# Where a doubled bias is added to an accumulator: on VectorE in eight pieces, or on GpSimd in four

## The chip, the cores and the metric

The kernel runs on one core of a Trainium2 chip. The metric is device time in microseconds (us), from the launch of the program to its end on the core. A core has five engines with an instruction queue each: TensorE (matrix products; PE in the profile, with the loading of weights shown apart as PEld), VectorE (DVE), ScalarE (ACT), GpSimd (POOL) and SyncE (SP, which here only starts transfers). TensorE writes its results to PSUM; the other working memory is SBUF. A queue is worked through in order, and an instruction waits on semaphores for what it needs from other engines and from transfers.

## What is computed

Cut to what matters, with x of 1024 x 512, weight of 64 x 512 x 512, all in fp32:

```python
out_lin = x @ lin_w.T + lin_b
xv = einsum('bf,efm->bem', x, weight)
zp = einsum('bf,efm->bem', square(x), square(weight))
interaction = 0.5 * sum(square(xv) - zp, axis=1)
return out_lin + interaction
```

Per embedding e there is one product of x with a 512 x 512 matrix; the squares of all 64 products are summed. The sum over e of zp is one product of square(x) with the sum of the squared weights. The bias lin_b has 512 elements, one for each output column.

## The kernel before, in words

**Accumulator.** Two SBUF tiles, `acc[0]` and `acc[1]`, hold the upper and lower half of the output rows (index r), each as 128 partitions x 2 (j, blocks of 128 rows) x 2 (s, further blocks of rows) x 512 columns. They hold twice the result: the linear part is written to them doubled (lines 226, 303, 309), the squares are added, and the last stage multiplies by 0.5 (lines 688 and 713). So the bias too is added doubled.

**Main loop.** The 64 embeddings are worked in 16 groups q of 4. In a group the products are formed by a seven-product scheme (as Strassen's) at two levels: the outer blocks "1" to "7" each have an x side, made once, and a weight side, made by GpSimd for every group (`outer_t`, line 380; `inner_t`, lines 391, 393, 395). A `unit` (line 413) is one outer block i and one row half j: seven products on TensorE (line 421) into three PSUM banks x, v and y, ScalarE copies bank x into bank y (line 475), and VectorE adds the banks to what other units left in z tiles (lines 446, 457, 458 and the joins of line 467). For block "5" GpSimd adds two more pieces per j (`rest`, line 472). There are 14 units in a group. ScalarE squares the finished z tiles (`squares`, line 497), and a transfer from GpSimd's queue that adds to its destination gathers them into acc (`gather`, line 506). Squared weights are made by ScalarE (line 515) and summed in the same way (line 522). SP's queue loads the weights of the next group (line 358).

**What sets the order.** A timetable, written out by hand. Every step is put into `Stream` with a time (`st.at(t, fn)`), group q starts at 98q, and `run()` (line 23) issues all steps sorted by time. The times only set the order of the instructions in each engine's queue; when one runs is decided by its semaphores. One step of the timetable is one product. Near the change, on GpSimd's queue, in times from the start of a group: the gathers of z place "c" into acc[0] at 38.8 and 52.9, the inner weight sums of block "3" (tp, t6, t4) at 57.9, 58 and 61.7, the weight-sum transfer at 61.6, the two `rest` additions of the first j at 67 and 69.8, the gather of "c" into acc[1] at 73, the two `rest` additions of the second j at 74 and 76.8. The last gathers of the group before into acc[0] come at 12.3, into acc[1] at 26.2.

**The bias.** SP loads it, repeated over 128 partitions, into the SBUF tile `bias` (line 350, time -1). In groups 1 to 4 (n from 0 to 3) VectorE adds `2.0 * bias` to one piece of 128x512 of acc[0] at 27.6 and to one of acc[1] at 41.6 (`add_bias`, line 348); n gives the piece, j = n // 2 and s = n % 2. Eight instructions in all.

**The end.** After the last group comes the product of the squared x with the summed squared weights (lines 659 and 722), and stores.

Of the kernel before, what the change touches and what calls it, by code (L numbers as in the profile page):

```python
# [9 lines left out]
AF = mybir.ActivationFunctionType  # L10
ALU = mybir.AluOpType
# [17 lines left out]
def kernel(  # L29
# [31 lines left out]
    nc = tc.nc  # L61
    _, _, _, Q = x.shape
    E, F, M = weight.shape
    P = 128
# [16 lines left out]
    acc = [  # L81
        const.tile([P, 2, 2, M], F32, tag=f"acc{r}", name=f"acc{r}") for r in range(2)
    ]
# [26 lines left out]
    st = Stream()  # L110
# [232 lines left out]

    bias = const.tile([P, M], F32, tag="bias", name="bias")

    def add_bias(r, j, s):
        o = acc[r][:, j, s]
        nc.vector.scalar_tensor_tensor(o, bias, 2.0, o, ALU.mult, ALU.add)  # L348

    st.at(-1, lambda: nc.sync.dma_start(bias, lin_b.partition_broadcast(P)))  # L350

    for n in range(4):
        for r, t in enumerate((27.6, 41.6)):
            st.at(98 * (n + 1) + t, lambda r=r, n=n: add_bias(r, n // 2, n % 2))

    def load_w(q, kk, v):
        src = weight[4 * q + 2 * v : 4 * q + 2 * v + 2]
# [177 lines left out]
    for q in range(NQ):  # L535
# [29 lines left out]
        for k, n, r, times in (  # L565
# [5 lines left out]
            for j in range(2):  # L571
                t = g0 + 14 * k + 7 * j + 14.6
# [259 lines left out]
```

## Time and profile before

| | |
|---|---|
| time, median of 3 runs | 1425.74 us (1425.23 to 1425.85) |
| the profiled execution's own time | 1423.9 us |
| its span, first to last instruction | 1422.1 us |
| mean granted TensorE clock | 0.996 |
| TensorE busy | 1407.7 us (99%), 3340 instructions |
| VectorE busy | 893.6 us (63%), 1271 |
| ScalarE busy | 620.8 us (44%), 824 |
| GpSimd busy | 1248.8 us (88%), 812 |
| transfers that add z to acc (line 506) | 190 issues, median 8.5 us to landing for 512 KB |
| load of the bias (line 350) | 1 issue, 256 KB, 13.5 us to landing |

The profile is of one execution, so sums of its durations are to be set against 1423.9 us. A line of a timeline gives the start, the duration, the engine, the line of the code, the operation, output<-inputs by tile name, the shapes, and in brackets how long the engine had been idle before and what released it. In the list of waits the numbers are the total in us, how often, and the longest. A product of fp32 shows as two matmul records. Ends of matmuls are modelled, so successive records overlap.

### The profile page before, as it was taken

How to read it: one execution, taken by the hardware profiler on the slowest of the kernel's cores; microseconds unless marked ns; L12 is line 12 of the kernel's file. 1: busy time of each engine (PE TensorE's matmuls, PEld its weight loads, DVE VectorE, ACT ScalarE, POOL GpSimd, SP SyncE). 2: the span in 40 equal slices, each digit the busy share in tenths (PEclk: the TensorE clock that was granted, in tenths of full speed). 3: DMA queues.
4: the chain of work that ended last, by engine and by line, in shares of the span. 5: the costliest groups of instructions: out<-in, count | busy, mean ns of one | idle time of the engine just before them, and what ended most of it. 6: DMA issues, size and time to landing. Idle time of an engine off the chain costs nothing.

```text
span 1422.1 us, 11166 instructions
## 1 busy us (share of the span) xinstructions
PE 1407.7 (99%) x3340; PEld 636.5 (45%) x3340; DVE 893.6 (63%) x1271; ACT 620.8 (44%) x824; POOL 1248.8 (88%) x812
## 2 busy tenths in 40 slices
PE   9999999999999999999999999999999999999999
PEld 5444444444444444444444444444444444444446
DVE  6665667657576565665656566565666656566665
ACT  2444353443534435344443534534353443534443
POOL 7988789888898888979989898988989988898984
PEclk9999999999999999999999999999999999999999
DMA  5299898898888998997998899898998998899885
GB/s 214 59 222 191 200 197 160 200 195 195 197 163 206 196 206 193 182 238 156 230 195 197 204 181 234 166 232 178 191 233 160 225 195 211 186 184 237 163 189 133
DMA packets 58108, 273.63 MB, mean 192 GB/s; under 512 B 5440, under 2 KB 8000, under 8 KB 41792
## 3 DMA queue, kind: packets, MB, share of 16 engines
q0 software_dynamic: 36432, 198.20, 71.1%
q1 hardware_dynamic: 21328, 74.19, 15.3%
q10 hardware_dynamic: 288, 0.52, 0.1%
q8 instruction: 27, 0.44, 0.1%
q14 instruction: 33, 0.27, 0.1%
HBM read 72.61 MB, written 2.10 MB: 53 GB/s over the span
## 4 chain that ended last, share of the span: by engine, by line
PE 94%; DMA 2%; issue 1%; POOL 1%; DVE 1%; ACT 0%; POOLq 0%
PE y L421 39%; PE x L421 26%; PE v L421 25%; DMA acc<-z 2%; PE lin L216 1%; PE y_last L659 1%; DVE acc L348 1%; PE v_last L659 0%; PE x_last L659 0%; POOL t L380 0%; PE y_lin L271 0%; DMA t<-lin_wT 0%; POOL t L395 0%; PE v_lin L271 0%; PE x_lin L271 0%
## 5 line engine op out<-in xcount | busy, mean ns | idle before, releaser
L421 PE MATMUL y<-t,xs 128*128 128x512 f32 x896 | 424.0, 594 | 10.3 <-DVE z L467 9.6
L475 ACT COPY y<-x 128x512 f32<-128x512 f32 x224 | 127.7, 570 | 623.1 <-PE x L421 623.0
L467 DVE TENSOR_TENSOR z<-y,s 128x512 f32<-128x512 f32 x192 | 132.7, 691 | 238.0 <-PE y L421 238.0
L421 PEld LDWEIGHTS y<-t,xs 128*128 128x128 f32 x896 | 169.7, 190 | 226.7 <-issue 202.8
L506 POOL DMA_DIRECT2D acc<-z x190 | 213.2, 1153 | 64.3 <-DMA acc<-z 62.7
L497 ACT ACTIVATE z<-z 128x1024 f32<-128x1024 f32 x256 | 260.1, 1054 | 11.8 <-POOL z L472 9.3
L421 PE MATMUL x<-w,xs 128*128 128x512 f32 x512 | 252.0, 600 | 0.0
L421 PE MATMUL y<-tp,xs 128*128 128x512 f32 x448 | 229.1, 593 | 0.0
L421 PE MATMUL v<-tp,xs 128*128 128x512 f32 x448 | 228.8, 592 | 0.0
L472 POOL TENSOR_TENSOR z<-z,s 128x1024 f32<-128x1024 f32 x64 | 149.6, 2355 | 50.7 <-DVE s L467 50.7
L421 PE MATMUL x<-t,xs 128*128 128x512 f32 x384 | 188.3, 592 | 0.0
L391 POOL TENSOR_TENSOR tp<-w 128x1024 f32<-128x1024 f32 x64 | 175.2, 2738 | 13.9 <-PE y L421 12.6
L467 DVE TENSOR_TENSOR z<-v,s 128x512 f32<-128x512 f32 x192 | 132.8, 691 | 72.2 <-PE v L421 70.6
L458 DVE TENSOR_TENSOR z<-y,z 128x512 f32<-128x512 f32 x192 | 132.4, 690 | 57.4 <-PE y L421 57.4
L380 POOL TENSOR_TENSOR t<-w,t 128x1024 f32<-128x1024 f32 x64 | 164.1, 2725 | 0.0
L458 DVE TENSOR_TENSOR z<-x,z 128x512 f32<-128x512 f32 x192 | 132.3, 689 | 37.3 <-PE x L421 35.7
L421 PEld LDWEIGHTS x<-w,xs 128*128 128x128 f32 x512 | 98.4, 192 | 123.8 <-issue 123.5
L391 POOL TENSOR_TENSOR tp<-t 128x1024 f32<-128x1024 f32 x48 | 139.5, 2906 | 0.0
L421 PEld LDWEIGHTS y<-tp,xs 128*128 128x128 f32 x448 | 85.6, 191 | 107.8 <-issue 107.8
L421 PEld LDWEIGHTS v<-tp,xs 128*128 128x128 f32 x448 | 85.1, 190 | 107.3 <-issue 104.2
L421 PE MATMUL v<-w,xs 128*128 128x512 f32 x256 | 130.7, 592 | 0.0
L446 DVE TENSOR_TENSOR s<-v,z 128x512 f32<-128x512 f32 x160 | 110.6, 691 | 27.8 <-PE v L421 27.1
(113 smaller groups left out, 1485.0 us busy)
## 6 DMA issues: line engine op xcount, KB each, us to landing
w<-weight SPq DMA_DIRECT2D x64, 1024.0 KB, 12.8
acc<-z POOLq DMA_DIRECT2D x128, 512.0 KB, 8.5
w_sum<-w_sb POOLq DMA_DIRECT2D x63, 1024.0 KB, 10.2
acc<-z POOLq DMA_DIRECT2D x62, 1024.0 KB, 8.7
w<-x SPq DMA_DIRECT2D x2, 1024.0 KB, 10.2
out<-z SPq DMA_DIRECT2D x7, 256.0 KB, 2.3
xs<-x SPq DMA_DIRECT2D x2, 384.0 KB, 6.9
t<-lin_wT ACTq DMA_DIRECT2D x2, 256.0 KB, 4.2
```

The lines of the kernel that those rows point to most:

```text
L216: nc.tensor.matmul(LIN[n], quarter(0, kk, (0, 1, 3, 2)[2 * s + l])[:, ts(j, P)], lw_sb[:, 2 * kk + l, :], start=(kk == 0 and l == 0), stop ...
L348: nc.vector.scalar_tensor_tensor(o, bias, 2.0, o, ALU.mult, ALU.add)
L380: nc.gpsimd.tensor_sub(OUTER[i][:, u], a[:, u], b[:, u])
L391: nc.gpsimd.tensor_sub(t, b[:, 1], b[:, :, 0])
L421: nc.tensor.matmul(d[bank], xsl(i, o)[:, ts(j, P)], operand_b(q, i, o), start=start, stop=True, skip_group_check=True,)
L446: nc.vector.tensor_add(o, d[bank], zblk(q, addend, j, b))
L458: nc.vector.tensor_add(zblk(q, dst, j, b), d[bank], zblk(q, addend, j, b))
L467: nc.vector.tensor_add(s if both else zblk(q, dst, j, b), d[bank], s)
L472: nc.gpsimd.tensor_add(place(q, n)[:, 1, j], place(q, src)[:, 1, j], d["s"])
L475: st.at(t0 + 0.5, lambda: nc.scalar.copy(d["y"], d["x"]))
L497: lambda u=u: nc.scalar.activation(z[:, u, j], z[:, u, j], AF.Square),
L506: nc.gpsimd.dma_start(o, z, accum_op=ALU.add)
```

## The change

The tile `bias` is doubled in place, once, by ScalarE at time 21. The addition to acc moves from VectorE to GpSimd: in place of eight instructions of 128x512 at 27.6 and 41.6 there are four of 128x1024 at 64.5 of groups 1 to 4, each for one r and one j and both s, with the bias read twice over by a step of 0. n now gives r = n // 2 and j = n % 2. The load of the bias stays as it is.

```diff
-    def add_bias(r, j, s):
-        o = acc[r][:, j, s]
-        nc.vector.scalar_tensor_tensor(o, bias, 2.0, o, ALU.mult, ALU.add)
+    def add_bias(r, j):
+        o = acc[r][:, j]
+        nc.gpsimd.tensor_add(o, o, bias.unsqueeze(1).broadcast_to([P, 2, M]))
 
     st.at(-1, lambda: nc.sync.dma_start(bias, lin_b.partition_broadcast(P)))
+    st.at(21, lambda: nc.scalar.activation(bias, bias, AF.Copy, scale=2.0))
 
     for n in range(4):
-        for r, t in enumerate((27.6, 41.6)):
-            st.at(98 * (n + 1) + t, lambda r=r, n=n: add_bias(r, n // 2, n % 2))
+        st.at(98 * (n + 1) + 64.5, lambda n=n: add_bias(n // 2, n % 2))
```

## Prediction

> **What bounds the kernel now.** I read the page's busy shares first, then the waits of TensorE, then the lines that the diff removes, then the timelines around one of them. The shares:
>
> ```profile
> PE 1407.7 (99%) x3340; PEld 636.5 (45%) x3340; DVE 893.6 (63%) x1271; ACT 620.8 (44%) x824; POOL 1248.8 (88%) x812
> ```
>
> TensorE is the bound; a change elsewhere counts only where TensorE waits for it. Its waits are few:
>
> ```profile
> PE y L421 <- DVE z L467: 9.6, 4, 2.7
> PE y_spin L202 <- PEq L821: 0.8, 1, 0.8
> PE y L421 <- POOL t L395: 0.7, 1, 0.7
> ```
>
> So four gaps, 9.6 us in all, wait for a VectorE join (L467). What makes that join late is the removed line:
>
> ```profile
> L348 DVE SCALAR_TENSOR_TENSOR acc<-bias,acc x8: 1371/3518/5667, 138.3 to 414.0; 128x512 f32<-128x512 f32 x8
> ```
>
> Eight of them, 1.37 to 5.67 us each, where VectorE's other 128x512 operations take 0.69. Around the second one (VectorE, then TensorE, then GpSimd; columns: start, duration in us, engine, line):
>
> ```profile
> 149.63 0.69 DVE L458 TENSOR_TENSOR z<-x,z 128x512 f32<-128x512 f32 x1 [0.17 <-PE x L421]
> 150.24 5.31 DVE L348 SCALAR_TENSOR_TENSOR acc<-bias,acc 128x512 f32<-128x512 f32 x1
> 155.47 0.68 DVE L467 TENSOR_TENSOR z<-y,s 128x512 f32<-128x512 f32 x1
> ```
>
> ```profile
> 152.86 1.02 PE L421 MATMUL y<-t,xs 128*128 128x512 f32 x2
> 156.20 1.20 PE L421 MATMUL y<-t,xs 128*128 128x512 f32 x2 [2.32 <-DVE z L467]
> 157.19 3.55 PE L421 MATMUL x<-w,xs 128*128 128x512 f32 x4
> ```
>
> ```profile
> 150.22 1.56 POOL L395 TENSOR_TENSOR t<-w,t 128x512 f32<-128x512 f32 x1
> 151.44 1.18 POOL L522 DMA_DIRECT2D w_sum<-w_sb  x1
> 152.04 2.94 POOL L391 TENSOR_TENSOR tp<-t 128x1024 f32<-128x1024 f32 x1
> ```
>
> L348 starts at 150.24, just behind GpSimd's L395 (150.22), and ends at 155.55, about 0.6 us after GpSimd's L391 (154.98): it stood still while GpSimd worked, then did its 0.69 us. The join queued behind it came at 155.47, TensorE had a gap of 2.32 us, and the next four matmuls took 3.55 us where four in a row elsewhere take 1.88.
>
> **What the Trainium skill says.** "SBUF — State Buffer", section "Who interferes with whom": a VectorE instruction with two SBUF inputs contends with a GpSimd instruction that reads SBUF, and the later one blocks until the first is done; with at most one SBUF input (and outside the two-port modes) it does not contend. The trace agrees: L348 reads bias and acc, both in SBUF, and stretches to 5.31 us; the joins and sums read one operand from PSUM and hold 0.69 us. It goes a little beyond the page: the 0.26 us between L395's end (151.78) and L391's start did not let L348 in. "TensorE: Matmul & The Clock Gate", section "What's actually happening", makes the clock depend on how busy the array has been; the slow matmuls after the gap agree, and the page's clock is otherwise full.
>
> **What each stall costs.** The ScalarE copy y<-x (L475) runs once per unit of seven products, so its starts in ScalarE's timeline are a ruler:
>
> ```profile
> 144.48 0.57 ACT L475 COPY y<-x 128x512 f32<-128x512 f32 x1 [3.47 <-PE x L421]
> ...
> 150.49 0.57 ACT L475 COPY y<-x 128x512 f32<-128x512 f32 x1 [1.63 <-PE x L421]
> 160.78 0.57 ACT L475 COPY y<-x 128x512 f32<-128x512 f32 x1 [9.72 <-PE x L421]
> ```
>
> A unit takes 6.01 us (144.48 to 150.49), but the one with L348 takes 10.29: 4.28 lost. The other three such units read from the same timeline are 9.96 (and 6.31 for the unit after it), 8.58 and 10.44: 4.25, 2.57 and 4.43 lost. Sum 15.53. Cross-check: the first copies of weight groups 1 to 5 stand at 114.44, 202.84, 291.21, 377.90 and 466.77, so those four groups take 352.33 us; groups 5 to 9 take 84.12 each, four of them 336.48. Difference 15.85, of which 0.32 is a wait in group 4 for GpSimd. So the removal can return about 15.5 us.
>
> **The change, part by part.**
> (a) Removed: 8 VectorE L348. The first of each group (1.37 to 1.75 us) makes no TensorE gap: worth nothing. The second makes all four gaps: minus 15.5 us. What is late next there? In groups 5 to 15 the same place runs without L348 at 6.01 us per unit, so nothing is waiting behind it.
> (b) Added: one ScalarE activation on bias, 128x512. ScalarE's acc<-lin rows of this form take 0.60 us; "ScalarE: Activation LUTs", section "What ACT_TABLE_LOAD costs", gives 186 ns plus 0.833 per element, an estimate of 0.61. At 21 of the timetable it stands between two copies of the first group:
>
> ```profile
> 46.63 0.58 ACT L453 COPY z<-y 128x512 f32<-128x512 f32 x1 [1.75 <-PE y L421]
> 48.40 0.57 ACT L475 COPY y<-x 128x512 f32<-128x512 f32 x1 [1.19 <-PE x L421]
> ```
>
> ScalarE idles 1.19 us there, so 0.61 fits. Its new wait is for the bias load, issued by SP at 9.9 and landed after 13.5 us, at 23.4: long past. Uncovered, it would delay one y<-x copy by at most 0.61 us, once. Cost 0.
> (c) Added: 4 GpSimd adds of 128x1024 at 98(n+1)+64.5, so behind t4 of block 3 (61.7) and ahead of the first "rest" addition (67). The same place in group 5, which has no stall in it, on GpSimd:
>
> ```profile
> 512.31 0.86 POOL L506 DMA_DIRECT2D acc<-z  x1
> ...
> 520.00 1.56 POOL L395 TENSOR_TENSOR t<-w,t 128x512 f32<-128x512 f32 x1
> 524.26 4.68 POOL L472 TENSOR_TENSOR z<-z,s 128x1024 f32<-128x1024 f32 x2 [2.69 <-DVE s L467]
> ```
>
> GpSimd idles 2.69 us, waiting for VectorE. A 128x1024 addition with two SBUF inputs takes 2.35 (two L472 in 4.68) when no DMA issue stands just ahead, 2.64 when one does (the L380 behind the gather at 512.31). Here none does: 520.00 + 1.56 + 2.35 is 523.91, ahead of 524.26, so I take 2.35 and cost 0. With 2.64 the margin is 0.05, still no loss. The repeated bias operand is a form that no row shows. From below, nothing makes the add useful to anyone sooner, so no gain; from above I keep the rivals. Its new waits are for the doubled bias (long done) and, in groups 1 and 2, for the gather of acc[0] issued at 512.31: those at 249.66, 512.31 and 681.75 landed in 8.0, 8.1 and 9.0 us, i.e. by 521.3 at the latest, against t4's end at 521.56. For acc[1] the last gather is 38 timetable units older. Behind the add on GpSimd stand the two rest additions, the gathers of "c" and the weight sums; VectorE waits for rest "a" about 2 us after it ends (524.26 + 2.35 = 526.6, the reader starts at 528.64).
> (d) Nothing is moved past the DMAs of GpSimd's queue except the add itself; SP's queue is unchanged.
>
> **Sum.** The profiled execution took 1423.9 us (span 1422.1 and 1.8 around it): 1423.9 - 15.5 + 0 + 0 = 1408.4. The median of the runs is 1425.74, 1.84 above. The third stall lacked the slow matmuls (2.57 against about 4.3, so 1.75 less), which by itself explains that difference if in the other runs all four have them; those runs then lose 17.3, and 1425.7 - 17.3 is 1408.4 again.
>
> **The rivals.**
> R1, the add spills: with the gather landing late (its longest landing in the trace is 14.1 us) or the add longer than 2.69, rest and the gathers slip and the next group's operands come late. For it: GpSimd is 88% busy and in group 7 its idle stretch is only 1.71. Against it: 2.56 to 2.70 in the others, and 0.55 more before the second pair. The largest loss that late GpSimd operands cause in any group is 0.92 us (group 11); four of these are 3.7: 1412.1.
> R2, something else ends at the same place: the gaps shrink but VectorE's join stays late. Against it, groups 5 to 15. If only half the loss goes, 7.75: 1423.9 - 7.75 = 1416.2.
> R3, slower: the add's operand that repeats over two blocks is read at a third of the speed, 7.1 us. Then 7.1 - 2.69 = 4.4 us per group go straight through rest, gather and next operands; 4 x 4.4 = 17.6 against 15.5, so 1426.0, about no change. It turns slower by over 0.2% from an add of 7.3 us (4.6 x 4 = 18.4); at 8.5 us it gives 1408.4 + 4 x 5.8 = 1431.6. Nothing in the trace speaks for it.
> R4, the change does nothing measurable: excluded unless VectorE keeps two-SBUF operations in these groups, which the diff does not leave.
>
> **How the numbers follow.** Forecast (stalls gone, add hidden) 0.78, R1 0.13, R2 0.04, R3 0.05 (0.03 of it about no change, 0.02 slower). Forecast's own spread: 1406.8 if the 0.32, 0.34 and 0.92 us waits of groups 4, 8 and 11 are also missing, 1410.2 if the 1.84 between profile and median stays. With R1 the range is 1406.5 to 1412.5. A measurement here can tell about 0.2% (2.9 us): faster 0.95, within 0.2% 0.03, slower 0.02.
>
> **What would show it.** Groups 1 to 4 at 84.1 us each; no TensorE wait for DVE z L467; VectorE without any operation above 0.7 us between 60 and 1400 us; four GpSimd adds of about 2.35 us, the idle time before the rest pair down to about 0.2; ScalarE's doubling at about 47 us. I am wrong if these adds exceed 2.7 us or wait for acc<-z, or if groups 1 to 4 stay above 85 us.

## The result, and the profile after

The changed kernel takes 1407.25 us (median of 4 runs, 1406.88 to 1407.61) against 1425.6 before: ratio 0.9871, 95% interval 0.9854 to 0.9889. The forecast was 1408.4. The profiled execution took 1406.91 us (span 1405.1), 17.0 less than the one before.

The page's busy shares, after:

```profile
PE 1400.6 (100%) x3340; PEld 634.7 (45%) x3340; DVE 869.1 (62%) x1263; ACT 621.2 (44%) x825; POOL 1256.9 (89%) x816
```

TensorE's waits, after (total, times, longest):

```profile
PE y_spin L202 <- PEq L821: 0.8, 1, 0.8
PE y L421 <- POOL t L395: 0.5, 1, 0.5
```

The four waits for a VectorE join are gone, and no other has come in their place. The instructions that touch `bias`, after:

```profile
L348 POOL TENSOR_TENSOR acc<-acc,bias x4: 2629/2638/2647, 167.7 to 420.5; 128x1024 f32<-128x1024 f32 x4
L350 SPq DMA_DIRECT2D bias<-lin_b x1: 466/466/466, 9.7 to 9.7; - x1
L351 ACT ACTIVATE bias<-bias x1: 633/633/633, 45.9 to 45.9; 128x512 f32<-128x512 f32 x1
```

The ruler of ScalarE's copies around the same place of group 1, after:

```profile
143.27 0.57 ACT L475 COPY y<-x 128x512 f32<-128x512 f32 x1 [3.47 <-PE x L421]
...
149.28 0.57 ACT L475 COPY y<-x 128x512 f32<-128x512 f32 x1 [1.63 <-PE x L421]
155.29 0.57 ACT L475 COPY y<-x 128x512 f32<-128x512 f32 x1 [5.44 <-PE x L421]
```

The unit that took 10.29 us takes 6.01. Groups 1 to 4 take 84.12, 84.12, 84.11 and 84.45 us, together 336.80; before it was 352.33, so 15.53 less. The 0.33 that group 4 takes more than the others is a wait that it had before too. The other 1.5 of the 17.0 can't be put down to the change: the ruler's first copy stands at 31.56 instead of 32.76 (1.2; in the experiments below it stands anywhere from 31.6 to 32.7, with and without the gain), and 0.3 lies in small waits of groups 11 and 12, which also differ from run to run.

Where the additions went, on GpSimd in group 1, after:

```profile
166.47 1.57 POOL L395 TENSOR_TENSOR t<-w,t 128x512 f32<-128x512 f32 x1
167.70 2.64 POOL L348 TENSOR_TENSOR acc<-acc,bias 128x1024 f32<-128x1024 f32 x1
170.72 4.68 POOL L472 TENSOR_TENSOR z<-z,s 128x1024 f32<-128x1024 f32 x2 [0.39 <-DVE s L467]
```

The rest pair still waits for VectorE, 0.39 us instead of 2.69: the addition ends before it is in anyone's way. Its 2.64 us are read with care: the record starts 0.34 before t4's ends (166.47 + 1.57 = 168.04), and from there it is 2.30.

### The profile page after: what moved, and what is told of

Read it like the earlier page. It is cut to its first block, busy times and chain, and to the rows that moved or that the text cites. A ratio compares the mean times of both kernels' runs of the same rounds, so it can differ in the third digit from the quotient of the medians.

```text
span 1405.1 us, 11169 instructions
## 1 busy us (share of the span) xinstructions
PE 1400.6 (100%) x3340; PEld 634.7 (45%) x3340; DVE 869.1 (62%) x1263; ACT 621.2 (44%) x825; POOL 1256.9 (89%) x816
## 3 DMA queue, kind: packets, MB, share of 16 engines
q1 hardware_dynamic: 21328, 74.19, 15.5%
## 4 chain that ended last, share of the span: by engine, by line
PE 96%; DMA 2%; POOL 1%; issue 0%; ACT 0%; DVE 0%; POOLq 0%; ACTq 0%
PE y L421 40%; PE x L421 27%; PE v L421 26%; DMA acc<-z 2%; PE lin L216 1%; PE y_last L659 1%; PE v_last L659 0%; PE x_last L659 0%; POOL t L380 0%; PE y_lin L271 0%; PE y_spin L202 0%; POOL t L395 0%; PE x_lin L271 0%; PE v_lin L271 0%; POOL tp L391 0%
## 5 line engine op out<-in xcount | busy, mean ns | idle before, releaser
L421 PE MATMUL x<-w,xs 128*128 128x512 f32 x512 | 248.4, 592 | 0.0
L391 POOL TENSOR_TENSOR tp<-w 128x1024 f32<-128x1024 f32 x64 | 175.4, 2741 | 3.7 <-PE y L421 2.4
L391 POOL TENSOR_TENSOR tp<-t 128x1024 f32<-128x1024 f32 x48 | 139.5, 2907 | 0.0
```

The source lines that it names most:

```text
L391: nc.gpsimd.tensor_sub(t, b[:, 1], b[:, :, 0])
L421: nc.tensor.matmul(d[bank], xsl(i, o)[:, ts(j, P)], operand_b(q, i, o), start=start, stop=True, skip_group_check=True,)
```

## The experiments

Each kernel is the changed kernel with one more change, unless said otherwise. Times are medians; in brackets stand the ratio to the kernel before, run beside it, and its 95% interval. The theory: at 41.6 an addition with two SBUF inputs stands still while GpSimd works, the join queued behind it is late, and TensorE waits. According to it, all else is free.

**1 and 2: half of the move each.** The VectorE addition comes back for one half of acc only (bias doubled by ScalarE).

```diff
+    def add_vec(r, j, s):
+        o = acc[r][:, j, s]
+        nc.vector.scalar_tensor_tensor(o, bias, 1.0, o, ALU.mult, ALU.add)
...
+    for n in range(4):                                            # 1: acc[0] at 27.6; 2: acc[1] at 41.6
+        st.at(98 * (n + 1) + 27.6, lambda n=n: add_vec(0, n // 2, n % 2))
+    for n in range(2):
+        st.at(98 * (n + 1 + 2) + 64.5, lambda n=n: add_bias(1, n))
```

> The additions to acc[0] are back on VectorE at 27.6 in groups 1 to 4 (bias already doubled), those to acc[1] stay on GpSimd at 64.5. Theory (only the additions at 41.6 cost, since two GpSimd instructions run over them): about 1407.3, groups 1 to 4 at 84.1 us each, the four VectorE additions at 1.4 to 1.8 us each with no TensorE gap. Rival (VectorE's total work or every one of its blocked additions costs, so half of the move brings half of the gain): about 1416.

> The other half: the additions to acc[1] are back on VectorE at 41.6 in groups 1 to 4, those to acc[0] stay on GpSimd at 64.5 in groups 1 and 2. Theory: all of the gain is lost, 1423.5 to 1426, four TensorE gaps of about 2.3 us for the join of line 467, additions of about 5.3 us. Rival (half and half): about 1416.

Measured: 1 took 1407.87 us (0.9883, 0.9867 to 0.9900), 2 took 1423.27 (0.9993, 0.9983 to 1.0002), just below the range expected. VectorE's additions in 1, then in 2 (ns, shortest, median, longest):

```profile
L352 DVE SCALAR_TENSOR_TENSOR acc<-bias,acc x4: 1371/1382/1758, 138.1 to 390.8; 128x512 f32<-128x512 f32 x4
```

```profile
L352 DVE SCALAR_TENSOR_TENSOR acc<-bias,acc x4: 5278/5338/5667, 149.7 to 415.3; 128x512 f32<-128x512 f32 x4
```

So the loss is at 41.6; at 27.6 an addition may be blocked for 0.7 us (once 1.1) and TensorE does not notice. "Half and half" falls.

**3: VectorE keeps all eight, at another place.**

```diff
-    for n in range(4):
-        st.at(98 * (n + 1) + 64.5, lambda n=n: add_bias(n // 2, n % 2))
+    for n in range(8):
+        st.at(98 * (n + 1) + 64.6, lambda n=n: add_vec(n // 4, n // 2 % 2, n % 2))
```

> All eight additions stay on VectorE as one instruction of 128x512 with two SBUF inputs, but one in each of groups 1 to 8 at 64.6, where GpSimd has nothing to do. Theory (the place decides, not the engine): 0.69 us each, no TensorE gap, 1407.3. Rival (work on VectorE between the joins delays them wherever it stands): joins late by 0.7 to 5 us in eight groups, 1415 to 1440.

Measured 1407.67 us (0.9882, 0.9867 to 0.9896). The additions in it:

```profile
L352 DVE SCALAR_TENSOR_TENSOR acc<-bias,acc x8: 681/681/855, 169.9 to 759.1; 128x512 f32<-128x512 f32 x8
```

The same instruction on the same engine is free where GpSimd is idle (in group 7, where GpSimd's t4 still ran for the first 0.3 us, it took 0.85). It is the place that cost, not VectorE.

**4: the doubling alone.** Additions at 27.6 and 41.6 on VectorE, as `nc.vector.tensor_add(o, o, bias)`.

> Only the doubling by ScalarE is kept; the eight additions are on VectorE at their old places, as plain additions of two SBUF tiles. Theory: no gain, 1425.6, additions of 1.4 and 5.3 us as before. Rival (the form with a scalar is what makes VectorE slow, and the doubling is what helps): additions of 0.7 us, about 1407.

Measured 1424.91 us (0.9998, 0.9990 to 1.0007):

```profile
L348 DVE TENSOR_TENSOR acc<-acc,bias x8: 1390/3542/5664, 137.1 to 413.2; 128x512 f32<-128x512 f32 x8
```

Whether the instruction multiplies by a scalar or only adds plays no part.

**5: one PSUM input at the old place.** In groups 1 to 4, at 41.6, a VectorE instruction of the old size on acc[1], besides the change. It adds nothing to acc, and the bank x is that of the unit in work.

```diff
+    def add_nothing(j, s, bank):
+        o = acc[1][:, j, s]
+        nc.vector.scalar_tensor_tensor(o, bank, 0.0, o, ALU.mult, ALU.add)
...
+        if i == "6" and j == 1 and 1 <= q <= 4:
+            st.at(t0 + 6.6, lambda: add_nothing((q - 1) // 2, (q - 1) % 2, d["x"]))
```

> The changed kernel with four more VectorE instructions, at the old place 41.6 in groups 1 to 4 and of the old form and size, on acc[1], but with one input from PSUM (0 times the bank x of the unit, plus acc). Theory (two SBUF inputs beside GpSimd's reads make the stall): 0.69 us each, no TensorE gap, 1407.3. Rival (any extra VectorE work at this place, or any access to acc there, makes it): 1415 to 1425.

Measured 1407.50 us (0.9892, 0.9875 to 0.9908):

```profile
L352 DVE SCALAR_TENSOR_TENSOR acc<-x,acc x4: 681/681/681, 149.7 to 402.4; 128x512 f32<-128x512 f32 x4
```

Same place, same size, same accumulator, and 0.68 us instead of 5.3. The second SBUF input is what makes VectorE wait. That it waits for GpSimd is read from experiment 3 and from the ends of the additions, which follow the ends of GpSimd's instructions (10 and 11); no run takes GpSimd's work away at 41.6 itself. Experiment 5 also rules out that the old addition waited for a gather into acc[1].

**6: how long may VectorE be held there?** The instruction of experiment 5, g times in group g, for g from 1 to 8.

> The changed kernel with g more VectorE instructions at 41.6 of group g, for g from 1 to 8, each 0 times the bank x plus acc (one PSUM input, 0.61 to 0.69 us). It measures how long VectorE may be held at this place before TensorE loses time. Theory (the stall is nothing but the time that the join waits in VectorE's queue; the slack is 5.31 - 2.32 = 3.0 us of inserted work): groups 1 to 4 at 84.1, group 5 about 84.2, groups 6, 7 and 8 lose 0.7, 1.3 and 1.9 us and in some of them up to 1.9 more by a slower clock after the gap. Rival (the lock does more harm than its duration): no loss up to 8, or another slope than one to one.

Measured 1418.08 us (one run). The block of g instructions lasts 0.68, 1.40, 2.13, 2.86, 3.58, 4.30, 5.03 and 5.76 us. TensorE's gaps, in groups 5 to 8 (TensorE's timeline of this kernel; there are none in groups 1 to 4):

```profile
490.43 1.13 PE L425 MATMUL y<-t,xs 128*128 128x512 f32 x2 [0.59 <-DVE z L471]
...
576.12 1.12 PE L425 MATMUL y<-t,xs 128*128 128x512 f32 x2 [1.31 <-DVE z L471]
...
662.54 1.73 PE L425 MATMUL y<-t,xs 128*128 128x512 f32 x2 [2.04 <-DVE z L471]
...
751.39 1.83 PE L425 MATMUL y<-t,xs 128*128 128x512 f32 x2 [2.76 <-DVE z L471]
```

Read off these gaps, the slack is 2.99 us each time (3.58 - 0.59, 4.30 - 1.31, 5.03 - 2.04), and beyond it TensorE loses one for one. The ruler gives less. By it the four units lose 0.86, 1.57, 4.00 and 4.72 us, and the unit of group 4, in which no gap shows, loses 0.13:

```profile
402.20 0.57 ACT L479 COPY y<-x 128x512 f32<-128x512 f32 x1 [1.63 <-PE x L425]
408.34 0.57 ACT L479 COPY y<-x 128x512 f32<-128x512 f32 x1 [5.57 <-PE x L425]
```

These are 6.14 us in place of 6.01. In groups 4, 5 and 6 the block less the loss is the same, 2.86 - 0.13, 3.58 - 0.86 and 4.30 - 1.57: a slack of 2.73. The ends of matmuls are modelled, so the first 0.26 us of a gap do not show as one; in group 4 the time lies in a record of four matmuls that reads 2.01 us, where 1.88 is usual. The losses exceed the expected ones because an instruction more lasts 0.72 us here, not 0.61 to 0.69, and because the expected slack had been read off a gap too. In groups 7 and 8 the slack explains 2.30 and 3.03 us; about 1.7 us more are lost in each. That is the clock, in a window behind each of the four gaps (window, its length, TensorE's busy time and matmuls, granted clock, share of the transfer engines, GB/s):

```profile
490.40:494.00 3.60, 3.57 (x9) 1.00 0.89 182
576.00:580.00 4.00, 3.88 (x9) 1.00 0.97 197
662.50:666.00 3.50, 3.46 (x5) 0.56 1.08 220
751.00:755.00 4.00, 3.61 (x5) 0.58 1.09 223
```

**7: is the addition on GpSimd really free?** One in each of groups 1 to 12, each of 2/3 of the bias.

> The changed kernel with one GpSimd addition at 64.5 in each of groups 1 to 12 in place of 1 to 4 (bias scaled by 2/3, so the sum is the same). Theory (the addition is fully covered by GpSimd's wait for VectorE): 1407.3, no change to the changed kernel within 0.5. Rival (it costs a little each time that the noise hides): eight more of them show, at 0.3 us each 1409.7, at 0.9 us each 1414.5.

Measured 1407.65 us (0.9893, 0.9873 to 0.9913): eight more additions move nothing that can be told from the noise.

**8: what a spill costs.** Two, then three additions per group in groups 1 to 12 (1/3 and 2/9 of the bias each).

```diff
+    for n in range(12):
+        for m in range(2):                                        # or 3
+            st.at(98 * (n + 1) + 64.5 + 0.1 * m, lambda n=n: add_bias(n // 2 % 2, n % 2))
```

> Two GpSimd additions at 64.5 in each of groups 1 to 12 (bias scaled by 1/3), so that GpSimd's work there runs about 2.0 us past its idle time (idle left 0.39, one addition more takes 2.35). This prices the spill of the rivals R1 and R3. Reading of R3 (an overshoot goes straight through): 2.0 us less 0.55 of the second gap in each of 12 groups, about 17 us more, 1425. Reading of R1 (what is behind it has slack of its own): at most 0.9 us per group, 1407 to 1418.

> Three GpSimd additions at 64.5 in each of groups 1 to 12 (bias scaled by 2/9): 2.35 us more of GpSimd's time per group than with two. If an overshoot goes straight through, the loss per group rises from 1.15 to 3.5 us, and the time to about 1453. If the delay is made good elsewhere in a group, less: 1430 to 1445.

Measured: 1424.83 us with two (1.0000, 0.9994 to 1.0007), so 17.6 over the changed kernel, 1.46 per group; 1455.17 with three (one run), 4.0 per group. GpSimd with two, in group 5:

```profile
510.43 5.07 POOL L348 TENSOR_TENSOR acc<-acc,bias 128x1024 f32<-128x1024 f32 x2
515.46 4.69 POOL L473 TENSOR_TENSOR z<-z,s 128x1024 f32<-128x1024 f32 x2
520.07 0.87 POOL L507 DMA_DIRECT2D acc<-z  x1
520.67 4.96 POOL L473 TENSOR_TENSOR z<-z,s 128x1024 f32<-128x1024 f32 x2
```

Both idle stretches are gone. One addition more is 2.35 us, 0.39 were left: 1.96 over, and less the 0.55 of the second stretch 1.41 should be lost. The 1.46 measured is an average over unequal groups. By the ruler most lose 1.15, a part of it in the second unit of the next group; group 7, whose first idle stretch was shorter already before (1.71), loses about 2.8, and group 11 about 2.5, which is not explained.

A third addition brings the overshoot, less the second stretch, to 3.76. The 4.0 measured hold something else besides: in six of the twelve groups the 13th unit takes 9.42 to 9.44 us, in the other six 7.73, with TensorE's gap in it about 2.0 us in all of them. The difference of 1.7 is the clock again, as behind the gaps of groups 2 and 5:

```profile
276.40:280.40 4.00, 3.97 (x6) 0.62 0.55 109
542.10:546.10 4.00, 4.00 (x10) 1.00 0.57 111
```

Without it the loss is about 3.1 per group. So some four fifths of an overshoot go through to TensorE, with two additions (in most groups) as with three. TensorE's waits in the kernel with three show the way:

```profile
PE v L422 <- POOL tp L392: 23.9, 12, 2.0
PE y L422 <- DVE s L447: 4.2, 12, 1.6
PE y L422 <- POOL t L396: 2.9, 6, 0.5
```

It comes by way of the weight sums that stand behind the rest pairs (first and last line), and in part by VectorE, which waits for the first rest result (second line).

**9: the same additions where GpSimd is dense.** `64.5` becomes `42.5`.

> The four GpSimd additions stand at 42.5 instead of 64.5, ahead of the inner weight sums of block 5, where GpSimd has no idle time, and in groups 1 and 2 behind a gather into the same half of acc that has just been issued. Theory (the place is what makes it free): in groups 3 and 4 2.4 us of delay, of which GpSimd's small idle times take up to 0.3, so 0 to 2 us per group; in groups 1 and 2 a wait of about 5 us for acc<-z besides, 3 to 7 us per group; together 1413 to 1425. Rival (GpSimd has slack anywhere): 1407.3.

Measured 1419.48 us (0.9971, 0.9963 to 0.9980). The first addition, on GpSimd's timeline:

```profile
151.40 1.18 POOL L522 DMA_DIRECT2D w_sum<-w_sb  x1
156.69 2.35 POOL L348 TENSOR_TENSOR acc<-acc,bias 128x1024 f32<-128x1024 f32 x1 [4.11 <-DMA acc<-z]
```

In groups 1 and 2 the whole queue stood 4.1 to 4.4 us for the gather into acc[0]. A part of each addition's cost shows only in the second unit of the next group; counted with it, and without the 0.33 that group 4 loses anyway, the four additions cost 4.4, 4.7, 1.5 and 0.4 us by the ruler. The last two are those of groups 3 and 4, where nothing waits for a gather and only the 2.35 us of work are in the way. So "on GpSimd" gains only a part (6 us of 18); the place gives the rest.

**10 and 11: why GpSimd runs over the addition twice at 41.6.** There the addition stayed out over t4 (L395) and tp (L391). In 10 the eight additions are on VectorE at eight other places (24.6, 34.6, 76.6, 83.6, then 39.6, 45.6, 48.6, 55.6). In 11, experiment 2 is repeated with the weight-sum transfer, which is issued between t4 and tp, put behind tp.

```diff
-                t + (3.2 if t < 0 else 5),
+                t + (3.2 if t < 0 else 6.15 if 1 <= q <= 4 and (v, u) == (1, 0) else 5),
```

> All eight additions on VectorE, as instructions of 128x512 with two SBUF inputs, each at another place of the timetable: 24.6, 34.6, 76.6, 83.6 (acc[0], groups 1 to 4), 39.6, 45.6, 48.6, 55.6 (acc[1], groups 5 to 8). It asks how long GpSimd holds VectorE off. Reading A (the block ends with the GpSimd instruction that was running): no addition over 2.35 + 0.69 = 3.0 us, no TensorE gap, 1407.3. Reading B (the next GpSimd instruction keeps it off if it follows within a gap of about 0.3 us, as at 41.6): additions that last until the first longer gap in GpSimd's timeline, some over 3.7 us, and where one ends over 3.0 us late a TensorE gap of the excess, 1409 to 1420.

> As the kernel with the additions to acc[1] on VectorE at 41.6 and the others on GpSimd, but in groups 1 to 4 the weight-sum transfer of GpSimd's queue stands behind the tp sum of block 5 instead of ahead of it, so that GpSimd's two instructions that ran over the addition follow each other with no transfer issued between them. Reading C (the transfer issue between them is what lets GpSimd go on to the second): additions of about 2.1 us, no TensorE gap, 1407.5. Reading D (the state in which VectorE arrives at the first one decides, whatever follows): additions of 4 to 5.3 us and gaps of 1 to 2.3 us as before, 1412 to 1424.

Measured: 10 took 1408.89 us (one run). Its additions last 0.68 to 2.65 us, and each blocked one ends 0.55 or 0.56 after the end of the one GpSimd instruction that was running, as here in group 6 (577.58 against 577.02):

```profile
575.75 1.83 DVE L352 SCALAR_TENSOR_TENSOR acc<-bias,acc 128x512 f32<-128x512 f32 x1
574.06 2.96 POOL L395 TENSOR_TENSOR tp<-t 128x1024 f32<-128x1024 f32 x1
```

That is reading A at these places, but not without a loss: behind the longest (24.6, 2.65 us) TensorE waited 0.5 us for a VectorE sum, and its unit took 0.79 more. The slack at that place is 1.86 by the ruler, less than at 41.6. 11 took 1415.02 us (0.9942, 0.9925 to 0.9958); VectorE's addition and GpSimd's instructions in group 1 of it:

```profile
149.28 4.39 DVE L352 SCALAR_TENSOR_TENSOR acc<-bias,acc 128x512 f32<-128x512 f32 x1
```

```profile
149.26 1.55 POOL L401 TENSOR_TENSOR t<-w,t 128x512 f32<-128x512 f32 x1
150.49 2.62 POOL L397 TENSOR_TENSOR tp<-t 128x1024 f32<-128x1024 f32 x1
152.77 1.17 POOL L528 DMA_DIRECT2D w_sum<-w_sb  x1
```

It is again blocked over both (153.11 is tp's end, 153.67 the addition's), without a transfer issue between them, so reading C falls. The block is 0.9 us shorter, since tp starts earlier, so its end follows the end of GpSimd's work. The unit takes 1.66 us more, which is 4.39 - 2.73.

Why it is held over two instructions at 41.6 stays open. In 11 tp does not depend on t4, and its record starts 0.32 before t4's ends; but in the kernel before, tp starts 0.26 after t4's end, and the addition was held as well. What all sixteen additions at 41.6 (before, and experiments 2, 4 and 11) have in common is that they arrive while GpSimd is issuing a gather, just ahead of t4. In group 1 of the kernel before, where the addition starts at 150.24:

```profile
149.62 0.87 POOL L506 DMA_DIRECT2D acc<-z  x1
```

In group 4 of that kernel the addition's record even starts 0.35 us ahead of t4's, and it was held over both all the same. The blocked additions of 10, and those at 27.6, arrive while an instruction of GpSimd's is running. No run tried this difference by itself.

## Why the prediction was right, point by point

**The stall and its size (a).** Right. 15.53 us were read off the ruler, and groups 1 to 4 returned 15.53. The steps hold one by one: the second SBUF input (experiment 5), GpSimd's work as the other party (3, 10 and 11), only the second addition of each group (1, 2), nothing late next (84.12 us per group). That the 15.53 agree to the last digit says that nothing was left of the stalls and nothing new came; both figures rest on the same execution before. Another execution of the kernel before loses more or less than 15.5, as the clock falls behind all four gaps or not (next point).

**The slow matmuls.** A hold of 5.28 to 5.67 us less the slack of 2.73 gives 2.55 to 2.94, and the third stall lost just that (5.30 - 2.73 = 2.57). The others lost 1.5 to 1.7 more, and so did all four in experiment 2 and three of four in experiment 4. The estimate that the median's extra 1.84 us are one more such piece is well supported: in the runs of the kernel before taken beside the experiments the time goes with the granted clock of the run, 1424.5 to 1427.2 us at 0.995, 1423.1 to 1424.2 at 0.996, 1421.1 to 1421.8 at 0.998. The runs of the changed kernel are all at 1.0 and within 0.7 us. In the third stall before, the windows around the gap and behind it are at full clock; in the first they are not:

```profile
154.00:158.00 4.00, 1.80 (x3) 0.89 0.98 197
158.00:160.00 2.00, 2.00 (x4) 0.50 1.29 262
330.00:334.00 4.00, 1.69 (x5) 1.00 0.98 197
334.00:338.00 4.00, 4.00 (x11) 1.00 0.97 197
```

**ScalarE's doubling (b).** Right: 0.63 us against 0.61, at 45.91, and 0.66 us of idle time are left before the next copy.

**GpSimd's addition (c).** Right in its end and its cost, wrong in the record: forecast 3.91 us from the start of t4 to the end of the addition, measured 3.87; the record reads 2.64 instead of 2.35, because it begins under t4. (c) took 2.35 since no transfer issue stands just ahead; but one stands ahead of t4, and behind it the records overlap. Read by durations alone, my sign "about 2.35" would have looked missed. The idle time left, by the sum of (c) 0.35, is 0.39; the sign's "about 0.2" did not follow from that sum. The bias operand that is read twice over costs nothing extra (2.35 us in experiment 9), and no wait for acc<-z came up.

**The rivals.** R1's price was wrong: I capped the loss of a spill at 0.92 us per group, the largest that this trace happened to hold. Experiment 8 measures 1.15 in most groups for an overshoot of 1.96, and 3.1 for one of 4.3, the clock left out. R3's rule, that an overshoot goes straight through, was the better one; with the 0.55 us of the second stretch taken off it is about a fifth too high. So the margin was as forecast, but there is no cap behind it. In experiment 7 some of the margin was left in eleven of the twelve groups (0.25 to 0.39 us); in group 7 there was none, the second stretch took up the rest, and the group still took 84.12 us.

**The 1.2 us.** The forecast was 1.5 us too high for the profiled execution and 1.15 for the median. In the profiled executions 1.2 us are the start-up before the first unit, which moves from run to run with no link to the change and was long in the one before; I had no term for it. The other executions were not profiled, so for the median this is likely and not shown. In the spread, the low end of 1406.8 counted group 8's wait of 0.34, which its next unit made good already before (6.35, then 5.73).

## What to carry to other kernels

Look at an instruction that is much longer than others of its size, ask what it shares with the engine that works beside it, and then ask who is queued behind it: here 0.7 us of work cost 4 us because a join stood behind it. Price such a wait by the slack in front of the bounding engine (here nothing up to 2.7 us, one for one beyond, and 1.7 us more where the clock fell), not by the length of the wait; and read the slack off a ruler, since a short gap can hide under modelled ends. When work moves to a busy engine, the free stretch it is put in counts more than the engine: the same four additions cost nothing in one stretch and 12 us at another place, and VectorE itself did them for nothing in the stretch where GpSimd was idle.

## What the runs showed of the hardware that was not expected

- VectorE, held off by GpSimd, gets in at the end of the running GpSimd instruction in most places and is done about 0.55 us after it, but stayed out over two GpSimd instructions at 41.6 in every group tried (5.3 to 5.7 us, and 4.4 to 4.7 when the second began earlier).
- Where VectorE gets in, GpSimd's next instruction pays: in experiment 10 sums of 128x512 that last 1.27 us elsewhere last 1.61 to 1.72 behind it.
- After gaps of up to 1.74 us (experiments 6 and 11) TensorE's clock stayed full. After gaps of 2.0 to 2.8 us it fell in most cases, to between 0.5 and 0.75 over some microseconds, mostly at a loss of 1.7 us; but it stayed full after one of 2.31 us before, one of 2.33 in experiment 4, and six of twelve of about 2.0 in experiment 8. So the length of the gap alone does not decide.
- GpSimd's records overlap where an instruction does not need the one before. With no transfer issue near, by 0.05 us or less (in experiment 9 tp's starts at 159.01, and the addition's ends at 159.04); behind an issue, by 0.34 (t4 and the addition, after) or 0.65 (experiment 9, group 3).
